# Adding x to the output rows: an accumulating transfer from DRAM in place of a load and GpSimd's additions

## Chip, cores and metric

The kernel runs on one core of one Trainium2 chip. The metric is the device time of one execution in microseconds (us). The engines are named as in the profile: PE is TensorE's matmul, PEld its weight load, DVE is VectorE, ACT is ScalarE, POOL is GpSimd, and SP is SyncE, which here only issues transfers. A "q" behind a name (SPq) stands for the engine's sequencer.

## What is computed

A cross attention over B = 64 independent items. Item b has text rows x[b] (256 x 512) and context rows c[b] (256 x 384). All is in float32.

```
text_p  = x @ W_text  + b_text           # 256 x 512
audio_p = ctx @ W_audio + b_audio        # 256 x 512
Q = layer_norm(text_p, g1, beta1);  K = layer_norm(audio_p, g2, beta2);  V = audio_p
alpha = softmax(Q K^T / sqrt(512))       # 256 x 256
H = (alpha V) @ W_out + b_out            # 256 x 512
out = layer_norm(H + x, g_out, beta_out)
```

The last line is the one that matters here: x itself is added to the projected rows, ahead of the last layer norm.

## The kernel before

Each item is 256 rows, so two blocks of 128 partitions (LT = ST = 2). The order of instructions on every engine is written out by hand; each engine works through its own queue in that order, and waits by semaphore where an operand isn't there yet. A loop over b = 0 to 61 runs three items at once in one iteration: the scores and softmax of item b, the projections q and k of item b + 2, and the context, output projection and last layer norm of the items before b. In an iteration `at` is the attention of item b, `last` that of b - 1 and `done` that of b - 2. The last two items run behind the loop in code of their own.

The projections q, k and the output projection y are objects of class `Blocks`: PE computes seven half-width products (`products`, line 472) into PSUM, and DVE brings them out one after the other (`leave`, line 483) in the order 1, 6, 2, 5, 3, 7, 4. After `leave(3)` row block 0 of the result is complete, after `leave(4)` row block 1.

q and k are turned by way of DRAM. SP stores the rows (`store`, line 418: tiles qr to qd, kr to kd), fetches them again in 32-row squares by four transfers each (`fetch`, by `squares` at line 88: qq, kq), and DVE transposes the squares (lines 91 and 439). The softmax weights e take the same way (ed, eq). x and c are read twice: in squares (xq, cq) for the projections, and in rows (`load_rows`, lines 113 and 114) for the addition of x and for the context product.

The rows of x, `x_sb`, are a 512 KB tile of pool `xin` (three buffers). Item 0 has its own loads at line 157. The output rows y, tile `yr` (two buffers), go through these steps for `done`, in three places of an iteration:

- DVE: `leave(3)`, `leave(7)`, `leave(4)`; then POOL: `add_x` (line 593), one addition for each of the two row blocks. Next in POOL's queue are `sum_x` and `sum_c` of item b + 3 (`turn_next`), whose results are used an iteration later, then the 1/std of y.
- ACT: `statistics` (lines 601 and 606), two passes over each row block, first the mean and then the centred square sum. They stand in ACT's queue behind the exponentials and the division of e, and ahead of the squares of q, the copies of the context zT and the affine steps of qT and kT.
- DVE: `shift` (line 694) and `settle` (line 703), which overwrite y in place; between them stands the transpose of k. Behind them on DVE come the seven `leave` steps of k, then those of the next y. SP: `store` (line 713) writes y to the output.

The four last items (60 to 63) are finished behind the loop. For items 62 and 63 the rows of x are used in other ways too: POOL adds the output bias into them (`add_bias`), and DVE adds them as it brings the product out of PSUM (`evict`).

Of the kernel before, what the change touches and what calls it, by code (L numbers as in the profile page):

```python
# [9 lines left out]
F32 = mybir.dt.float32  # L10
AF = mybir.ActivationFunctionType
ALU = mybir.AluOpType
# [3 lines left out]
P = 128  # L16
# [6 lines left out]
def kernel(  # L23
# [41 lines left out]
    nc = tc.nc  # L65
    ctx.enter_context(tc.manual_schedule())
    B, L, D = x.shape
    S, DA = c.shape[1:]
    H = w_text.shape[1]
    LT, ST = L // P, S // P  # L70
# [4 lines left out]
    xin = ctx.enter_context(tc.tile_pool(name="xin", bufs=3))  # L75
# [32 lines left out]
        load_x(b)  # L108

    def load_rows(b):  # L110
        x_sb = xin.tile([P, LT, D], F32, tag="x", name=f"x_{b}")
        c_sb = cin.tile([P, ST, DA], F32, tag="c", name=f"c_{b}")
        nc.sync.dma_start(x_sb, x[b].rearrange("(t p) d -> p t d", p=P))
        nc.sync.dma_start(c_sb, c[b].rearrange("(t p) d -> p t d", p=P))
        return x_sb, c_sb

# [382 lines left out]
    class Attention:  # L499
# [89 lines left out]
            self.y = self.o.rows  # L589

        def add_x(self):
            for t in range(LT):
                nc.gpsimd.tensor_tensor(self.y[:, t, :], self.y[:, t, :], self.xb[:, t, :], ALU.add)  # L593

# [261 lines left out]
    for b in range(B - 2):  # L856
# [23 lines left out]
        if b + 4 < B:  # L880
            load_squares(b + 4)
        at.fetch_e()
        rows[b + 1] = load_rows(b + 1)
        if done:
            done.statistics()
# [59 lines left out]
    q[B - 1].fetch()  # L945
    k[B - 1].fetch()
    rows[B - 1] = load_rows(B - 1)
    at.scores()
    done.o.leave(3)
# [107 lines left out]
```

## Time and profile before

| | |
|---|---|
| median of 3 runs | 1422.26 us (1420.84 to 1422.74) |
| the profiled execution | 1420.47 us, its span 1418.7 us, granted clock 0.998 |
| busy time: PE, DVE, ACT, POOL | 1405.0, 1273.3, 931.8, 875.2 us |
| DMA | 322.61 MB, mean 227 GB/s; SP's queue occupies 80.4% of the 16 DMA engines |
| x in rows (line 113) | 63 transfers of 512 KB, median 3.9 us from issue to landing |
| additions of x (line 593) | 124, mean 1274 ns, 157.0 us busy |
| POOL's idle time ahead of them | 58.0 us, ended by DVE's last writes of y |

The span is the time from the first to the last instruction in the profile; the execution's own time lies 1.8 us above it, and this execution lies 1.8 us below the median. Each row of the profile is of one execution. A row such as `L593 POOL TENSOR_TENSOR yr<-yr,x` gives the line of the kernel, the engine, the operation, and the tile written and those read. The mean granted clock is TensorE's, as a share of full speed. The time from issue to landing runs from the instruction that issues a transfer to its semaphore.

### The profile page before, as it was taken

How to read it: one execution, taken by the hardware profiler on the slowest of the kernel's cores; microseconds unless marked ns; L12 is line 12 of the kernel's file. 1: busy time of each engine (PE TensorE's matmuls, PEld its weight loads, DVE VectorE, ACT ScalarE, POOL GpSimd, SP SyncE). 2: the span in 40 equal slices, each digit the busy share in tenths (PEclk: the TensorE clock that was granted, in tenths of full speed). 3: DMA queues.
4: the chain of work that ended last, by engine and by line, in shares of the span. 5: the costliest groups of instructions: out<-in, count | busy, mean ns of one | idle time of the engine just before them, and what ended most of it. 6: DMA issues, size and time to landing. Idle time of an engine off the chain costs nothing.

```text
span 1418.7 us, 23330 instructions
## 1 busy us (share of the span) xinstructions
PE 1405.0 (99%) x6441; PEld 1220.9 (86%) x6441; DVE 1273.3 (90%) x2134; ACT 931.8 (66%) x2293; POOL 875.2 (62%) x1295
## 2 busy tenths in 40 slices
PE   9999999999999999999999999999999999999997
PEld 5788888888888888888888888888888888888885
DVE  5889999999999999999999999999999999999987
ACT  4666676676676676766766766766767667667662
POOL 5557556666666666566566665666665755666645
PEclk9999999999999999999999999999999999999999
DMA  8898887887888788788878887887887888788763
GB/s 207 228 246 229 242 244 209 242 240 216 237 233 234 228 230 238 233 226 236 244 217 236 239 224 228 238 229 229 229 238 232 225 239 242 216 238 241 205 200 109
DMA packets 450582, 322.61 MB, mean 227 GB/s; under 512 B 154900, under 2 KB 382996, under 8 KB 450452
## 3 DMA queue, kind: packets, MB, share of 16 engines
q1 hardware_dynamic: 450356, 320.98, 80.4%
q8 instruction: 53, 0.87, 0.3%
q14 instruction: 77, 0.63, 0.2%
q10 hardware_dynamic: 96, 0.13, 0.0%
HBM read 204.09 MB, written 116.92 MB: 226 GB/s over the span
## 4 chain that ended last, share of the span: by engine, by line
PE 94%; DMA 2%; DVE 1%; POOL 1%; SPq 1%; issue 1%; ACT 0%; POOLq 0%; DVEq 0%; ACTq 0%
PE ps_q L472 26%; PE ps_y L472 21%; PE ps_k L472 20%; PE ps_sc L511 15%; PE ps_z L577 11%; DMA qq<-qd 0%; DMA xq<-in_x_dram 0%; DMA qd<-qr 0%; DMA wt<-in_L_xattn_W_text_dram 0%; SPq L150 0%; DMA bt<-in_L_xattn_b_text_dram 0%; POOL rstd L343 0%; POOL ve L341 0%; DVE qr L483 0%; DVE st L267 0%
## 5 line engine op out<-in xcount | busy, mean ns | idle before, releaser
L341 POOL TENSOR_SCALAR ve<-var 128x2 f32<-128x2 f32 x126 | 43.6, 346 | 310.8 <-ACT junk L380 310.8
L511 PE MATMUL ps_sc<-kT,qT 128*128 128x256 f32 x1024 | 231.7, 379 | 1.9 <-ACT kT L446 1.9
L528 ACT ACTIVATE e<-ps_sc,nmx 128x256 f32<-128x256 f32 x128 | 59.5, 469 | 245.7 <-DVE nmx L521 245.7
L483 DVE TENSOR_TENSOR qr<-ps_q,qr 128x512 f32<-128x512 f32 x378 | 188.1, 511 | 35.8 <-PE ps_q L472 23.3
L511 PEld LDWEIGHTS ps_sc<-kT,qT 128*128 128x128 f32 x1024 | 194.2, 190 | 29.6 <-ACT kT L446 2.9
L483 DVE TENSOR_TENSOR kr<-ps_k,kr 128x512 f32<-128x512 f32 x378 | 188.2, 512 | 24.7 <-PE ps_y L472 0.5
L483 DVE TENSOR_TENSOR yr<-ps_y,yr 128x512 f32<-128x512 f32 x372 | 185.1, 511 | 24.1 <-DVE yr L483 0.9
L593 POOL TENSOR_TENSOR yr<-yr,x 128x512 f32<-128x512 f32 x124 | 157.0, 1274 | 58.0 <-DVE yr L483 58.0
L577 PE MATMUL ps_z<-eT,c 128*128 128x256 f32 x768 | 176.5, 379 | 0.1
L472 PE MATMUL ps_q<-wtsum,xsum 128*128 128x256 f32 x756 | 173.6, 379 | 0.0
L343 POOL TENSOR_TENSOR rstd<-ve,nhalf 128x2 f32<-128x2 f32 (+1 forms) x194 | 158.9, 819 | 16.1
L472 PE MATMUL ps_k<-wa,cT 128*128 128x256 f32 x630 | 166.8, 379 | 0.0
L472 PE MATMUL ps_y<-wao,zT 128*128 128x256 f32 x620 | 164.2, 379 | 0.0
L577 PEld LDWEIGHTS ps_z<-eT,c 128*128 128x128 f32 x768 | 145.8, 190 | 20.7 <-ACT e L528 0.5
L472 PEld LDWEIGHTS ps_q<-wtsum,xsum 128*128 128x128 f32 x756 | 143.6, 190 | 19.9 <-POOL xsum L305 0.5
L380 ACT ACTIVATE junk<-kr 128x512 f32<-128x512 f32 x126 | 79.3, 629 | 96.8 <-DVE kr L483 96.8
L446 ACT ACTIVATE qT<-qT,columns 128x256 f32<-128x256 f32 x256 | 132.8, 591 | 8.3 <-DVE qT L91 8.3
L472 PEld LDWEIGHTS ps_k<-wa,cT 128*128 128x128 f32 x630 | 119.6, 190 | 16.2
L446 ACT ACTIVATE kT<-kT,columns 128x256 f32<-128x256 f32 x256 | 132.2, 589 | 1.1 <-DVE kT L91 0.9
L472 PEld LDWEIGHTS ps_y<-wao,zT 128*128 128x128 f32 x620 | 117.7, 190 | 16.0
L408 ACT ACTIVATE kr<-kr,rstd 128x512 f32<-128x512 f32 x126 | 84.1, 714 | 69.9 <-POOL rstd L343 69.9
L703 DVE SCALAR_TENSOR_TENSOR yr<-yr,rstd,beo 128x512 f32<-128x512 f32 x124 | 127.4, 1065 | 0.6 <-POOL rstd L343 0.6
(150 smaller groups left out, 2946.4 us busy)
## 6 DMA issues: line engine op xcount, KB each, us to landing
kd<-kr SPq DMA_DIRECT2D x64, 512.0 KB, 3.1
kq<-kd SPq DMA_DIRECT2D x256, 128.0 KB, 3.4
qd<-qr SPq DMA_DIRECT2D x64, 512.0 KB, 5.1
qq<-qd SPq DMA_DIRECT2D x256, 128.0 KB, 3.3
xq<-in_x_dram SPq DMA_DIRECT2D x252, 128.0 KB, 2.9
x<-in_x_dram SPq DMA_DIRECT2D x63, 512.0 KB, 3.9
out_dram<-yr SPq DMA_DIRECT2D x62, 512.0 KB, 5.0
cq<-in_ctx_dram SPq DMA_DIRECT2D x252, 96.0 KB, 2.5
```

The source lines that it names most:

```text
L341: nc.gpsimd.tensor_scalar(ve, var, EPS, None, ALU.add)
L343: nc.gpsimd.tensor_tensor(r, ve, nhalf[:, :n], ALU.pow)
L380: nc.scalar.activation(junk, self.rows[:, t, :], AF.Square, scale=1.0 / math.sqrt(H), accum_out=self.var[:, t : t + 1],)
L408: nc.scalar.mul(row, row, self.r[t])
L446: nc.scalar.activation(self.T[:, k, :], self.T[:, k, :], AF.Identity, bias=bet[:, k : k + 1], scale=gam[:, k : k + 1],)
L472: nc.tensor.matmul(bank[:, j, :], lhsT=side, rhs=w, start=(i == 0), stop=(i == len(pairs) - 1))
L483: add = lambda o, i0, i1: nc.vector.tensor_tensor(o, i0, i1, ALU.add)
L511: nc.tensor.matmul(self.sc[:, t, :], lhsT=self.qT[:, k, bass.ts(t, P)], rhs=self.kT[:, k, :], start=(k == 0), stop=(k == HC - 1),)
L528: nc.scalar.activation(self.e[:, t, :], self.sc[:, t, :], AF.Exp, bias=self.nmx[:, t : t + 1], accum_out=self.den[:, t : t + 1],)
L577: nc.tensor.matmul(ps[:, j, :], lhsT=self.c_sb[:, s, bass.ts(lo + j, P)], rhs=self.eT[:, s, :], start=(s == 0), stop=(s == ST - 1),)
L593: nc.gpsimd.tensor_tensor(self.y[:, t, :], self.y[:, t, :], self.xb[:, t, :], ALU.add)
L703: nc.vector.scalar_tensor_tensor(self.y[:, t, :], self.y[:, t, :], self.r[t], beo_sb, ALU.mult, ALU.add)
```

## The change

For items 0 to 59 the tile of x in rows is no longer allocated and no longer loaded. Where POOL added it, POOL now issues one transfer that reads x[b] from DRAM and adds it to y in SBUF. It covers both row blocks, 512 KB. The items 60 to 63 keep the load and the additions, and item 0 keeps its own loads at line 157, since its projection needs them.

```diff
     def load_rows(b):
-        x_sb = xin.tile([P, LT, D], F32, tag="x", name=f"x_{b}")
         c_sb = cin.tile([P, ST, DA], F32, tag="c", name=f"c_{b}")
-        nc.sync.dma_start(x_sb, x[b].rearrange("(t p) d -> p t d", p=P))
+        x_sb = None
+        if b >= B - 4:
+            x_sb = xin.tile([P, LT, D], F32, tag="x", name=f"x_{b}")
+            nc.sync.dma_start(x_sb, x[b].rearrange("(t p) d -> p t d", p=P))
         nc.sync.dma_start(c_sb, c[b].rearrange("(t p) d -> p t d", p=P))
         return x_sb, c_sb
...
         def add_x(self):
+            if self.b < B - 4:
+                rows_of_x = x[self.b].rearrange("(t p) d -> p t d", p=P)
+                nc.gpsimd.dma_start(self.y, rows_of_x, accum_op=ALU.add)
+                return
             for t in range(LT):
                 nc.gpsimd.tensor_tensor(self.y[:, t, :], self.y[:, t, :], self.xb[:, t, :], ALU.add)
```

## The prediction

> **What bounds the kernel now.** I read the page first, then stretches, then one iteration in the timeline, then the DMA engines in half-microsecond steps.
>
> ```profile
> span 1418.7 us, 23330 instructions
> PE 1405.0 (99%) x6441; PEld 1220.9 (86%) x6441; DVE 1273.3 (90%) x2134; ACT 931.8 (66%) x2293; POOL 875.2 (62%) x1295
> ```
>
> PE is busy 99% of the span. The view of busy time in three stretches says where the missing 13.7 us lie (columns: stretch, its length, busy time of PE, PEld, DVE, ACT, POOL, granted clock, DMA share, GB/s).
>
> ```profile
> 0.00:61.47 61.47, 56.94 (x213) 38.89 (x213) 42.10 (x71) 30.45 (x71) 33.63 (x60) 1.00 0.87 212
> 61.47:1378.30 1316.83, 1316.83 (x6100) 1158.84 (x6101) 1199.14 (x2007) 889.88 (x2197) 819.33 (x1212) 1.00 0.82 232
> 1378.30:1418.70 40.40, 31.25 (x129) 23.18 (x128) 32.07 (x58) 11.47 (x26) 22.26 (x25) 0.93 0.37 115
> ```
>
> From 61.47 to 1378.30 PE is never idle, at full granted clock. All idle time lies in the start (4.5 us) and the end (9.2 us). The timeline shows the period of the loop, by the first of the score products:
>
> ```profile
> 83.34 3.62 PE L511 MATMUL ps_sc<-kT,qT 128*128 128x256 f32 x16
> 104.93 3.62 PE L511 MATMUL ps_sc<-kT,qT 128*128 128x256 f32 x16
> 126.51 3.62 PE L511 MATMUL ps_sc<-kT,qT 128*128 128x256 f32 x16
> ```
>
> One iteration is 21.58 us of matmuls without a gap. Other work costs time only when it comes too late for PE; then it costs its lateness every iteration. So the question is how late x may land in y. These are the timeline's rows around the addition (start, length, engine, line); all are of the iteration at 709 to 731, but the last two, which repeat the end of the DVE work one period later.
>
> ```profile
> 710.60 2.52 POOL L593 TENSOR_TENSOR yr<-yr,x 128x512 f32<-128x512 f32 x2 [0.94 <-DVE yr L483]
> 711.05 0.36 SPq L418 DMA_DIRECT2D kd<-kr  x1
> 711.50 2.40 SPq L88 DMA_DIRECT2D qq<-qd  x4
> 714.20 1.78 SPq L88 DMA_DIRECT2D kq<-kd  x4
> 717.05 0.61 ACT L601 ACTIVATE junk<-yr 128x512 f32<-128x512 f32 x1
> 718.27 0.71 ACT L606 ACTIVATE junk<-yr,nm 128x512 f32<-128x512 f32 x1
> 720.85 1.37 DVE L694 SCALAR_TENSOR_TENSOR yr<-yr,nm,go 128x512 f32<-128x512 f32 x2
> ...
> 732.93 0.42 DVE L483 TENSOR_TENSOR yr<-ps_y,yr 128x256 f32<-128x256 f32 x1
> 733.27 0.70 DVE L91 STREAM_TRANSPOSE eT<-eq 128x512 f32<-128x512 f32 x1
> ```
>
> Two additions run back to back, the first as soon as row block 0 is complete. ACT comes to its statistics of y (L601) only at 717.05, 3.9 us after the additions end (713.12), and has no idle time there. Last, the DMA engines where the transfer would flow:
>
> ```profile
> 711.50:712.00 0.50, 0.50 (x4) 0.45 (x3) 0.50 (x2) 0.00 (x0) 0.50 (x2) 1.00 0.11 41
> 712.00:712.50 0.50, 0.50 (x5) 0.42 (x4) 0.50 (x2) 0.00 (x0) 0.50 (x1) 1.00 1.02 389
> 713.00:713.50 0.50, 0.50 (x4) 0.45 (x3) 0.50 (x2) 0.00 (x0) 0.12 (x1) 1.00 1.00 213
> ```
>
> They wake at about 711.9 for kd and are then full.
>
> **What is removed.** 59 loads of x (63 less those of items 60 to 63; item 0 has its own), 120 of 124 additions. The additions are 120 x 1.274 = 153 us of POOL, which is 62% busy and waited for by nobody here: worth 0. The loads are 0.40 us of issue on SP, worth 0 as SP waits behind them for DVE and ACT rows anyway. On the DMA engines each is 512 KB at about 400 GB/s = 1.3 us, between 725 and 730.5. Behind it c, out and qd land up to 1.3 us sooner; qd lands at 727.11 + 5.1 = 732.2 as it is, before its readers issue at 733.09: worth 0.
>
> **What is added.** 60 accumulating transfers, at the same place in POOL's queue. Three things differ from the additions.
>
> First, release. One transfer covers both row blocks, so it waits for the last DVE write of y, which ends at 732.93 + 0.42 - 21.58 = 711.77, not 710.60. Behind it on POOL wait sum_x and sum_c of a later item (used an iteration later, so covered) and the 1/std of this y, before which POOL idles 1.24 us. Issuing may take 2.52 + 0.54 + 1.24 = 4.3 us before that is late: 0.
>
> Second, the landing becomes a wait of ACT at L601. Call the time from release to landing L. Up to 717.05 - 711.77 = 5.3 us it costs nothing. Then ACT is late, and queued behind L601 are the squares of q, the two copies of zT that feed POOL's sums and PE's y products, and the affine steps of qT and kT. The y products have slack: POOL's second sum ends at 723.75, and PE reads it at 705.81 + 21.58 = 727.39, so 3.6 us. DVE has less. Its shift (L694) overwrites y and must wait for L606 of row block 0, which ends 718.98, so landing to shift is 718.98 - 717.05 = 1.93 us (1.95 with block 1). From the shift at 720.85 DVE works without an idle gap through the k rows to the last write of y at 733.35, 12.50 us. That write releases the next transfer. So there is a loop: L + 1.95 + 12.50 = L + 14.45. While L is below 21.58 - 14.45 = 7.13 us, PE sets the period; above it the loop does, and each microsecond costs 60 us.
>
> Third, L itself. No accumulating transfer and no transfer issued by GpSimd is in this trace, so each part is bounded.
> - Release to first data: kd, issued by SP at 711.05, moves data at 711.9, so 0.85 at least. At most GpSimd needs as long to write its list of rows as it took to add them: 0.85 + 2.52 = 3.4. I take 2.1, since POOL's smaller instructions take 0.5 to 1.2 us.
> - Data: x must be read and y must be read and rewritten. One pass is 1.3 us, two are 2.6. The engines are full with kd, qq and kq (shares 1.00 to 1.02); taking equal turns doubles 2.6 to 5.2. I take 4.7, nearer to the full rows.
> - Last data to landing: kd's data ends about 713.2 and it lands at 711.05 + 3.1 = 714.15, so 0.9; for x, 0.6.
>
> L = 2.1 + 4.7 + 0.9 = 7.7, with ends 0.85 + 1.3 + 0.6 = 2.75 and 3.4 + 5.2 + 1.0 = 9.6. The lower end is as good as the plain load of x (3.9 from issue to landing). The period is 7.7 + 14.45 = 22.15, 0.57 more, times 60 is 34 us.
>
> By the Trainium skill (DMA: Bandwidth & Descriptors, section Latency and other measured facts) a GpSimd transfer's first byte comes about 1 us after issue against 0.6 for SP. Estimated from that page's difference, the first part would be 0.85 + 0.4 = 1.25, L 6.85, and nothing would be lost. The same page's fit (section Anatomy of one DMA — SWDGE (gpsimd) path: 2.0 us and the bytes by 436 GB/s) would give 3.2 us for 512 KB, which the plain load's 3.9 in this trace already exceeds. I keep the rows' sum.
>
> The new traffic also delays kd, qq and kq by up to its 2.6 us. The last qq is issued at 713.45 and lands 3.3 later at 716.75; DVE turns it at 719.69, so 2.9 us of cover. The last kq lands at 715.53 + 3.4 = 718.9 and is turned at 722.14: 3.2. So 0, with 0.3 us to spare; if ACT is late by over 1.6 us, kd starts late as well and this cover goes too, but then DVE is late by itself.
>
> **The sum.** 1420.47 (span 1418.7) + 34 = 1454.5; the median of the runs is 1.8 above the profiled execution: 1456.
>
> **Rivals.**
> - No change: L stays under 7.13. For it: the plain load's 3.9, and 5.3 us that cost nothing at all. Against it: two reads, a full DMA, a later release. Time 1422, its own range 1420 to 1424.
> - The DMA engines become the bound. They are busy 0.82 x 21.58 = 17.7 us an iteration, which leaves 3.9, and 1.3 comes free with x. An accumulation that occupies them over 5.2 us breaks the period. Two passes at the 213 GB/s row are 4.9, so it takes a slower one than any row of this size; at 7.2 us the time is 2.0 x 60 = 120 us more, 1542.
> - Faster: GpSimd has 153 us less to do. PE has no idle gap in the loop to give, and start and end keep their loads and additions. Some 2 us at the edges at most: 1420 or less.
>
> **Chances.** The landing loop 0.53; DMA-bound 0.12; no change 0.32; faster 0.03. About 0.2% (2.8 us) is what a measurement of this kernel can tell from no change. Faster 0.03, same 0.32, slower 0.65. The forecast's range by L from 7.2 to 9.3 is 1426 to 1552; with the no-change case, 1419.5 to 1550. It leaves out the upper part of the DMA-bound case (0.06), L over 9.3 (0.08) and most of faster (0.02).
>
> **What would show it.** In the changed profile: PE's score products 22.1 us apart instead of 21.58 and PE idle; ACT waiting at L601 for a DMA into yr, longest in the list of waits; landing 7 to 8 us after issue; POOL some 150 us less busy; x loaded 4 times in 512 KB pieces. An unchanged 21.58 with ACT waiting little at L601 makes the forecast wrong in L; a DMA share near 1 in all windows means the second rival; kq or qq as what DVE waits for means that I misjudged the cover of the other transfers.

## The result, and the profile after

The changed kernel takes 1462.55 us (median of 6 runs, 1456.86 to 1467.37) against 1421.81 us before: a ratio of 1.0286, 95% interval 1.0271 to 1.0300, 41 us more. The profiled execution took 1456.86 us with a span of 1455.1, so it is the fastest of the six; what the profile shows is 36.4 us of span.

First the page: span, busy time, the two DMA queues (packets, MB, share of 16 engines), and three groups of instructions.

```profile
span 1455.1 us, 23096 instructions
PE 1421.1 (98%) x6441; PEld 1214.4 (83%) x6441; DVE 1247.0 (86%) x2134; ACT 921.9 (63%) x2293; POOL 771.9 (53%) x1235
...
q1 hardware_dynamic: 434308, 290.04, 77.2%
q0 software_dynamic: 16320, 31.46, 14.5%
...
L607 ACT ACTIVATE junk<-yr 128x512 f32<-128x512 f32 x120 | 74.5, 621 | 157.6 <-DMA yr<-in_x_dram 157.6
...
L596 POOL DMA_DIRECT2D yr<-in_x_dram x60 | 76.0, 1266 | 132.4 <-DVE yr L485 127.3
L91 DVE STREAM_TRANSPOSE qT<-qq 128x1024 f32<-128x1024 f32 x64 | 79.6, 1244 | 68.8 <-DMA qq<-qd 68.8
```

GpSimd's transfers have a queue of their own, and it occupies the engines for 14.5% of the span: 0.145 x 1455.1 / 60 = 3.5 us of all 16 engines per transfer. Two waits are new: ACT for the landing in yr (157.6 us) and DVE for the fetch of q (68.8 us, against 2.4 before). The stretch of the loop shows PE no longer without gaps, and fuller DMA engines (columns as before the change):

```profile
61.47:1410.00 1348.53, 1330.53 (x6090) 1150.68 (x6090) 1168.77 (x1999) 877.19 (x2192) 715.39 (x1150) 1.00 0.94 225
```

The starts of the first score product of the items are no longer 21.58 us apart: of the 57 in the loop's middle the median is 22.09 and the mean 22.16, single ones lie between 21.58 and 23.21. 60 x (22.16 - 21.58) = 35 us is nearly the whole difference of the spans. One iteration in the timeline:

```profile
702.63 3.62 PE L513 MATMUL ps_sc<-kT,qT 128*128 128x256 f32 x16
...
702.83 3.26 DVE L485 TENSOR_TENSOR yr<-ps_y,yr 128x512 f32<-128x512 f32 x6
705.71 0.36 SPq L420 DMA_DIRECT2D kd<-kr  x1
706.16 2.37 SPq L88 DMA_DIRECT2D qq<-qd  x4
706.40 1.26 POOL L596 DMA_DIRECT2D yr<-in_x_dram  x1 [2.08 <-DVE yr L485]
708.86 2.62 SPq L88 DMA_DIRECT2D kq<-kd  x4
713.60 0.63 ACT L607 ACTIVATE junk<-yr 128x512 f32<-128x512 f32 x1 [2.13 <-DMA yr<-in_x_dram]
714.47 1.25 DVE L91 STREAM_TRANSPOSE qT<-qq 128x1024 f32<-128x1024 f32 x1 [0.76 <-DMA qq<-qd]
714.84 0.71 ACT L612 ACTIVATE junk<-yr,nm 128x512 f32<-128x512 f32 x1
715.67 1.46 DVE L700 SCALAR_TENSOR_TENSOR yr<-yr,nm,go 128x512 f32<-128x512 f32 x2
724.30 3.26 DVE L485 TENSOR_TENSOR yr<-ps_y,yr 128x512 f32<-128x512 f32 x6
```

The last write of y ends at 702.83 + 3.26 = 706.09, GpSimd issues at 706.40, and ACT starts its statistics at 713.60: 7.5 us after the write here, 7.9 in the median. The shift follows ACT's start by 2.07 us (2.08 in the median). But just ahead of the shift DVE stands for 0.76 us before the turn of q, for a fetch that was issued from 706.16 on, side by side with the new transfer.

Which of the two comes last can be read from the start times. ACT's first centred pass (L612) ends at 714.84 + 0.71 = 715.55, and the shift starts 0.12 us later; behind the start of the turn it starts 1.20 later. Over the 57 iterations the shortest delays are 0.13 us behind ACT's pass and 1.17 behind the start of the turn. In 44 iterations the shift starts at the first of these, so ACT, and with it the landing, is what it waited for last; in 13 it is the turn of q. The margin is small: 0.2 us in the median, 0.6 at most. In the kernel before, the shift follows the turn in all 57, and ACT's pass has been over for 1.86 us (median). So the landing does hold up DVE, and the fetch of q is close behind. Whether the loss needs both is a question for experiments.

### The profile page after: what moved, and what is told of

It is laid out like the page before. It is cut to its first block, busy times and chain, and to the rows that moved or that the text cites. A ratio compares the mean times of both kernels' runs of the same rounds, so it can differ in the third digit from the quotient of the medians.

```text
span 1455.1 us, 23096 instructions
## 1 busy us (share of the span) xinstructions
PE 1421.1 (98%) x6441; PEld 1214.4 (83%) x6441; DVE 1247.0 (86%) x2134; ACT 921.9 (63%) x2293; POOL 771.9 (53%) x1235
## 3 DMA queue, kind: packets, MB, share of 16 engines
q0 software_dynamic: 16320, 31.46, 14.5%
## 5 line engine op out<-in xcount | busy, mean ns | idle before, releaser
L607 ACT ACTIVATE junk<-yr 128x512 f32<-128x512 f32 x120 | 74.5, 621 | 157.6 <-DMA yr<-in_x_dram 157.6
L341 POOL TENSOR_SCALAR ve<-ssq 128x2 f32<-128x2 f32 x60 | 39.6, 660 | 242.6 <-ACT junk L612 242.6
L343 POOL TENSOR_SCALAR ve<-var 128x2 f32<-128x2 f32 x126 | 27.5, 218 | 224.8 <-ACT junk L382 219.7
L596 POOL DMA_DIRECT2D yr<-in_x_dram x60 | 76.0, 1266 | 132.4 <-DVE yr L485 127.3
L91 DVE STREAM_TRANSPOSE qT<-qq 128x1024 f32<-128x1024 f32 x64 | 79.6, 1244 | 68.8 <-DMA qq<-qd 68.8
```

The source lines that it names most:

```text
L91: nc.vector.transpose(dst.rearrange("p k (b j) -> p b k j", j=SQ), src.rearrange("p b (k i) -> p b k i", k=chunks),)
L341: nc.gpsimd.tensor_scalar(ve, var, 1.0 / D, EPS, ALU.mult, ALU.add)
L343: nc.gpsimd.tensor_scalar(ve, var, EPS, None, ALU.add)
L596: nc.gpsimd.dma_start(self.y, rows_of_x, accum_op=ALU.add)
L607: nc.scalar.activation(junk, self.y[:, t, :], AF.Identity, scale=-1.0 / D, accum_out=self.nm[:, t : t + 1])
```

## Two loops, and experiments that tell them apart

Each wait closes a loop over iterations. The *landing loop* is the one of the prediction: last write of y, landing, statistics, shift, DVE's work up to the next last write. The *fetch loop* runs by way of SP: kd is issued, qq behind it, DVE turns q when qq has landed, works through k, ACT normalises k, and the next kd is issued. A loop sets the period when none of its links has slack left. Adding up its stretches doesn't show that: from one event to the same event an iteration later they make the period in any kernel, slack included. In the kernel before, kd to the turn of q is 8.64 us in the median and the turn to the next kd 12.95, the 21.58 that PE sets; only the link from qq to the turn is loose, as DVE practically never waits there, while ACT waits for the k rows of DVE. In the changed kernel both waits have changed. The rows of the lists of waits, of the kernel before and then of the changed one (waiting line, releaser, total us, times, longest):

```profile
ACT junk L380 <- DVE kr L483: 96.8, 120, 1.5
...
DVE qT L91 <- DMA qq<-qd: 2.4, 2, 1.8
```

```profile
DVE qT L91 <- DMA qq<-qd: 68.8, 61, 2.3
...
ACT junk L382 <- DVE kr L485: 5.4, 15, 0.5
```

So in the changed kernel the fetch loop isn't closed by itself: ACT, late by the landing, mostly comes to the k rows after DVE is done with them, so that the landing makes kd late as well. A third explanation is that the 16 DMA engines simply have too much to do. Times below are medians with the ratio to the kernel before of the same chip; periods are means of the same 57 iterations.

**The landing alone, without the traffic.** The kernel before, with one tiny transfer added:

```diff
         xs[b] = sum_x(xT.pop(b))
+        if done:
+            nc.gpsimd.dma_start(
+                done.y[:, :, :16],
+                x[done.b].rearrange("(t p) d -> p t d", p=P)[:, :, :16],
+                accum_op=ALU.add,
+            )
```

> The kernel before (loads of x, POOL's additions) with one more, tiny accumulating transfer into y, 16 columns of each row block (16 KB), issued by GpSimd behind the four sums of x, so that its landing is the last thing ACT's statistics wait for; these 16 columns get x twice. Hardly any traffic, but a late landing. It is issued about 716.5 on the scale of the profile before and lands 2.5 to 4.5 us later, 7.2 to 9.2 us after DVE's last write of y. Landing-loop theory: period = that time + 2.0 + 12.5, so 21.7 to 23.7, a time of 1430 to 1545, 1480 for a landing of 3.5 us. Traffic theory: 1420 to 1426.

Measured: 1517.67 us, ratio 1.0671 (1.0655 to 1.0686). The list of waits of this kernel:

```profile
ACT junk L601 <- DMA yr<-in_x_dram: 210.5, 59, 4.3
DVE yr L694 <- ACT junk L606: 133.7, 58, 3.0
```

ACT waits for the landing in 59 iterations, and DVE at the shift for ACT in 58. In each of the 57 iterations in the middle the shift starts 0.18 us behind ACT's pass, where the kernel before leaves 1.86. So no slack is left between them: ACT's statistics start 8.86 us after the last write of y (median), the shift 2.13 later, DVE needs 12.12 from there to the next last write, and the median period is 23.13. The landing loop exists and sets the period when the landing is that late, with 16 KB moved.

**The traffic alone, without the landing.** In the changed kernel the transfer goes to a dead tile, between two additions of a constant row:

```diff
-                nc.gpsimd.dma_start(self.y, rows_of_x, accum_op=ALU.add)
+                nc.gpsimd.tensor_tensor(self.y[:, 0, :], self.y[:, 0, :], bo_sb, ALU.add)
+                nc.gpsimd.dma_start(wo_sb[:, :LT, :], rows_of_x, accum_op=ALU.add)
+                nc.gpsimd.tensor_tensor(self.y[:, 1, :], self.y[:, 1, :], bo_sb, ALU.add)
```

> The changed kernel with its accumulating transfer sent to a dead region of SBUF of the same size (the first half of the tile of W_out), issued at the same place, between two additions on POOL that give y a constant row (the output bias) in place of x; so x is left out of the result. Same bytes, same issue, but nobody waits for the landing. Landing-loop theory: ACT waits for nothing at its statistics, the period is 21.58, the time 1420 to 1426. Traffic theory: DVE still waits about 1 us an iteration for qq, the time is 1440 to 1465.

Measured: 1448.71 us, ratio 1.0187 (1.0172 to 1.0202), period 22.04. Nobody waits for the landing, and two thirds of the loss are still there. Three rows of its list of waits and two of its timeline:

```profile
ACT junk L382 <- DVE kr L485: 91.0, 120, 1.4
...
DVE qT L91 <- DMA qq<-qd: 50.2, 60, 2.3
...
PE ps_y L474 <- DVE kr L485: 14.4, 24, 2.0
```

```profile
704.33 0.36 SPq L420 DMA_DIRECT2D kd<-kr  x1
...
713.34 1.25 DVE L91 STREAM_TRANSPOSE qT<-qq 128x1024 f32<-128x1024 f32 x1 [0.68 <-DMA qq<-qd]
```

DVE waits for qq in 60 iterations, ACT for DVE's k rows in all, and SP issues kd 0.03 us behind ACT's last row of k: the fetch loop is closed. kd to the turn of q takes 9.16 us in the median, in place of 8.64. PE then waits for DVE to empty PSUM. The shift follows the turn in all 57 iterations, with ACT's pass long over. The fetch loop is enough by itself.

**All of the change, but the landing has an iteration of time.** Statistics, shift, settle and store of an item are done one iteration later (every second y lies in the dead tile of W_out):

```diff
-        if done:
-            done.statistics()
+        if old:
+            old.statistics()
...
-        done, last = last, at
+        old, done, last = done, last, at
```

> The changed kernel with statistics, shift, settle and store of an item's y done one iteration later at the same places of the queues (every second y lies in the dead tile of W_out, so that there are four buffers); the item that is over at the end is finished just behind the loop. Same transfers at the same moments, but their landing has 21 us more. Landing-loop theory: no wait of ACT for the landing, period 21.58, time 1422 to 1432, of which up to 8 us is the extra item at the end. Traffic theory: the period stays 22.1, the time 1455 to 1470.

Measured: 1465.18 us, ratio 1.0306 (1.0291 to 1.0322), period 22.13. ACT's wait is gone and the period is that of the changed kernel. My theory of the landing loop fails here as the whole account of the loss: without that loop the loss is the same, but for 0.03 us an iteration, which is 2 us in all. DVE's wait for qq remained, nearly as large as in the changed kernel:

```profile
DVE qT L91 <- DMA qq<-qd: 64.6, 59, 2.0
```

And ACT waits for DVE's k rows again (83.9 us, 118 times), so without the landing the fetch loop closes and takes its place.

The time is above the changed kernel's although the period isn't, since the extra item at the end costs some 8 us: PE waits 8.0 us once for the transposed e there.

**Two transfers by row block.**

```diff
-                nc.gpsimd.dma_start(self.y, rows_of_x, accum_op=ALU.add)
+                for t in range(LT):
+                    nc.gpsimd.dma_start(self.y[:, t, :], rows_of_x[:, t, :], accum_op=ALU.add)
```

> The accumulation of each item as two transfers of 256 KB, one for each row block. Landing-loop theory (the time from DVE's last write of y to the landing, plus 2.08 us to the shift, plus 11.9 to 12.5 us of DVE work to the next last write of y, sets the period): block 0 is released 1.2 us earlier and has half the data, block 1 has half the data behind it. ACT's first pass starts 1 to 2 us sooner after the last write of y, 6 to 7 us in place of 7.9. The period falls to 21.6 to 21.7, the time to 1422 to 1430. Traffic theory (the added DMA work makes kd, qq and kq late, and DVE waits for them): the bytes are the same, so 1455 to 1465; and POOL issues twice, 2.5 us in place of 1.26, which could make it a little worse.

Measured: 1443.38 us, ratio 1.0154 (1.0138 to 1.0171), period 21.93. Neither number that was expected: ACT starts 5.28 us after the last write in the median, as in the kernel before, and still half of the loss remains, with DVE waiting 42.0 us for qq. The shift follows the turn of q in 56 of the 57 iterations, so what is left is the fetch's. How much of the gain comes from the earlier landing and how much from the earlier traffic isn't shown.

**A plain transfer in its place.**

```diff
-                nc.gpsimd.dma_start(self.y, rows_of_x, accum_op=ALU.add)
+                nc.gpsimd.dma_start(self.y, rows_of_x)
```

> The changed kernel with a plain transfer in place of the accumulating one, same place and size: x overwrites y, so the projection is left out of the result. Theory of two loops (landing: last write of y to ACT's statistics, plus 2.1, plus 11.9 to 12.2; fetch: kd's issue to the turn of q, which waits for qq behind it in the queue, plus 12.7): a plain transfer reads 512 KB less, so it lands 5.5 to 6.5 us after its start in place of 7.6, which takes the landing loop under 21.58, and qq comes back by 1.3 us or more, under 8.8 after kd: 1421 to 1430. If it is GpSimd's way of issuing (1.26 us of POOL and its own queue) and not the adding, the time stays 1450 to 1465.

Measured: 1423.24 us, ratio 1.0016 (1.0007 to 1.0025). Same queue, same bytes from DRAM, same wait, and the loss is all but gone: each of the 57 periods is 21.58. The rows of its page for GpSimd's queue and for the issue:

```profile
q0 software_dynamic: 8640, 31.46, 8.1%
...
L596 POOL DMA_DIRECT2D yr<-in_x_dram x60 | 47.9, 798 | 144.7 <-DVE yr L485 144.7
```

The engines are occupied 0.081 x 1422.8 / 60 = 1.9 us per transfer, against 3.5 for the accumulation; it lands 6.1 us after its start, against 7.6. The price of the change is thus the adding, not GpSimd's queue. The Trainium skill (Collectives: The Full Stack, section The bandwidth ceiling: the fold count and why AG ≠ RS ≠ AR) explains a reducing collective's lower rate by its two source reads and shows a ratio of 1.93 between a copying and an adding collective. Here the occupation by accumulating and plain transfers has a ratio of 3.5 / 1.9 = 1.8, which is near it; that the second read is the reason here too, no run shows.

**Three kernels with the fetch of q moved ahead of kd**, to break the fetch loop. The edit is the same in all; the kernels are the traffic-only one, the late one and the split one.

```diff
-            q[b + 1].fetch()
             k[b + 1].fetch()
...
         k2.normalise()
+        q2.fetch()
         k2.store()
```

> The traffic-only kernel (transfer into the dead tile, POOL adds the output bias in place of x) with the fetch of q moved ahead of the store of kd in SP's queue, so that qq no longer starts behind kd and beside the whole accumulation. Two-loops theory: the fetch loop is broken, the landing loop does not exist here, so the period is 21.58 and the time 1420 to 1428. Theory that the 16 DMA engines have too much to do (share 0.94): the order changes nothing, 1440 to 1450.

> The changed kernel with the statistics one iteration later and the fetch of q ahead of the store of kd: both loops broken, all the traffic and the accumulation into y kept. Two-loops theory: period 21.58 in the loop, time 1426 to 1434 (the extra item at the end costs about 8). Full DMA engines: 1455 to 1465.

> The accumulation in two transfers by row block (which brought ACT's statistics back to 5.3 us after the last write of y in its median) and the fetch of q ahead of the store of kd. Two-loops theory: both loops are at or under 21.58, time 1421 to 1432, the rest from iterations where block 1 lands late. Full DMA engines: 1440 to 1446 as without the move.

Measured: 1569.82 (ratio 1.1040, 1.1011 to 1.1068), 1579.05 (1.1122, 1.1089 to 1.1154) and 1551.32 us (1.0912, 1.0896 to 1.0928). All much slower, and neither theory had that. The list of waits of the traffic-only kernel, then of its SP queue:

```profile
DVE kT L441 <- DMA kq<-kd: 160.6, 60, 4.0
```

```profile
SPq L88 <- DMA kd<-kr: 377.8, 64, 7.9
SPq L88 <- DMA qd<-qr: 320.4, 64, 6.7
```

SP now stands before the fetch of q for qd's landing, with the store of kd queued behind it, and kd then shares the engines with qq and the accumulation (it lands after 6.8 us in place of 3.1), so kq, which must wait for kd, is what comes late. The move made a third loop in place of the second; it decides nothing about the second.

**The traffic moved in time.** The traffic-only kernel with its transfer issued behind the sums on POOL, some 7 us later, where the squares for a later item are being fetched:

```diff
             turn_next(b + 3)
+        if done and done.b < B - 4:
+            rows_of_x = x[done.b].rearrange("(t p) d -> p t d", p=P)
+            nc.gpsimd.dma_start(wo_sb[:, :LT, :], rows_of_x, accum_op=ALU.add)
```

> The traffic-only kernel (accumulation into the dead tile, POOL adds the output bias in place of x) with the transfer issued behind the sums of x and c on POOL, about 7 us later in the iteration, when qq and kq have been fetched and the squares of x and c for a later item are under way. The move of the fetch ahead of kd had failed as a test, since it put a wait for qd in front of kd and so made kq late; this one leaves SP's order alone. Fetch-loop theory: qq and kq are back at the turn in time, DVE waits for neither, period 21.58, time 1420 to 1428. Full DMA engines (0.94 to 0.96 busy whatever the order): 1440 to 1450.

Measured: 1422.22 us, ratio 1.0002 (0.9994 to 1.0011), each of the 57 periods 21.58. Its stretch of the loop and its rows for the two fetches (count, size, median from issue to landing):

```profile
61.47:1378.30 1316.83, 1315.46 (x6086) 1157.38 (x6087) 1197.76 (x2004) 890.28 (x2196) 890.78 (x1273) 1.00 0.95 231
```

```profile
kq<-kd SPq DMA_DIRECT2D x256, 128.0 KB, 3.4
...
qq<-qd SPq DMA_DIRECT2D x256, 128.0 KB, 3.2
xq<-in_x_dram SPq DMA_DIRECT2D x252, 128.0 KB, 6.2
```

The engines are 0.95 busy, as in the slow kernels, and nothing is lost: the explanation by full DMA engines falls. Now the fetches of x land late (6.2 in place of 2.9) and have an iteration to spare, and those of q and k are back at 3.2 and 3.4.

**Both at once, nothing left out.** The late kernel with its accumulation moved in the same way:

```diff
             done.o.leave(4)
-            done.add_x()
...
             turn_next(b + 3)
+        if done:
+            done.add_x()
```

> The kernel with the statistics one iteration later, the accumulation into y now issued behind the sums on POOL as in the traffic-only kernel of this set, and the steps of the extra item at the end put behind those of the next one. Nothing is left out: all accumulations, no wait for the landing, no collision with qq. Two-loops theory: 21.58 in the loop, time 1422 to 1430. Full DMA engines: 1450 to 1465.

Measured: 1427.78 us, ratio 1.0035 (1.0021 to 1.0049). Its loop is at 21.58 in each of the 57 periods; what is over comes from the extra item behind the loop, where the stretch from 1378.3 on is 47.7 us long instead of 40.4. With the late landing harmless and the traffic elsewhere, the accumulation costs nothing per iteration.

**Half of it.** SP loads the rows of block 1 alone, and block 0 gets x by the transfer:

```diff
+            nc.sync.dma_start(x_sb[:, 1, :], x[b, P:])
...
+                nc.gpsimd.dma_start(self.y[:, 0, :], rows_of_x[:, 0, :], accum_op=ALU.add)
+                nc.gpsimd.tensor_tensor(self.y[:, 1, :], self.y[:, 1, :], self.xb[:, 1, :], ALU.add)
```

> Half of the change: row block 0 gets x by an accumulating transfer of 256 KB, row block 1 by POOL's addition from a loaded half tile. Two-loops theory: the transfer is released 1.2 us earlier and occupies the engines about 1.8 us in place of 3.5, so it lands before ACT comes to its statistics, and qq is late by less than its cover: 1420 to 1426. If any accumulation costs in proportion to its bytes: half of the loss, 1440.

Measured: 1423.12 us, ratio 1.0013 (1.0004 to 1.0021). Half the bytes cost not half the loss but hardly anything: the price has a threshold, as both loops say. ACT waits 3.5 us in all for this transfer. No version beat the kernel before; its loop has no gap in PE to give back.

## Why the prediction was right, and where it was not

Forecast 1456, measured 1462.55; the loss was put at 34 us and is 41 in the median and 36 in the profiled execution. The reading of the profile held in most of its steps:

- PE sets the period of 21.58 and the 153 us of POOL are worth nothing: POOL is 103 us less busy (issuing takes 76) and no version is faster.
- The release waits for DVE's last write: POOL stands 127.3 us for it, in place of 58.0.
- The landing loop is at work in the changed kernel: ACT waits for the landing in all 57 iterations, the shift for ACT in 44, and the period is 22.16, as forecast (22.15).
- Its terms are off both ways, so that the sum fits this well is in part luck. L was put at 7.7 and is 7.9 in the median (7.97 in the mean). By the packets of GpSimd's queue, its parts are 2.9 us from release to first data, 4.5 of data and 0.5 to the landing, against 2.1, 4.7 and 0.9: the first was put 0.8 too short, the others together 0.6 too long. The other estimate of the first part, 1.25, by which nothing would have been lost, was further off. Landing to shift was 1.95 and is 2.08 (mean 2.11). The DVE stretch was 12.50 and is 11.9 (mean 12.10), mostly since the settle takes 1.37 where the row of before had 2.06.
- The rival of full DMA engines is refuted by the moved transfer, which keeps them 0.95 busy at no loss.

The step that failed is the cover of the other transfers: "So 0, with 0.3 us to spare". The accumulation was taken to occupy the engines 2.6 us, two passes of a plain one. It occupies them 3.5, more than the 2.9 us of cover that the turn of q had, and DVE now waits for qq 61 times. The prediction had named this sign of a misjudged cover itself. Priced at nothing, this step alone costs 27 us (the traffic-only kernel), and with the landing dependency taken away but the transfer at its real place, behind the last write of y, nearly the whole of the loss in the loop (the late kernel).

So the landing loop, which carried the forecast, is a real mechanism, but the loss doesn't need it. It is mostly last at the shift, by 0.2 us, and the fetch loop, which was left out of the sum, gives 22.13 in its place (the late kernel); lifting the landing alone therefore gained nothing. The prediction's remark that kd starts late as well when ACT is over 1.6 us late, "but then DVE is late by itself", fits what is seen: ACT waits 2.5 us for the landing in the median, and at the shift the fetch adds only 0.04 us to the mean iteration on top of it. What it missed is that the fetch comes late without the landing too. The number came out right without the fetch loop because the two happen to be nearly equally long; that wasn't foreseen, so this too is luck. What a kernel would take that had only the landing loop at this L was not tried. An estimate from its stretches in the changed kernel, L at its mean and the others at their shortest, is 7.97 + 2.07 + 11.89 = 21.93, or 21 us in 60 iterations.

## What to carry to other kernels

Where one engine sets the period without a gap, look for every loop that the change touches, not for the one that it lengthens: a new transfer has a landing that someone waits for, and a place in time at which it delays the transfers beside it. Write each loop as a sum of its links without their slack, each the shortest time from one release to the next, and compare it with the period (with the slack in them the stretches add up to the period in any kernel). In a profile, look at each place where two of them meet for the one that came last. A change is free as long as every loop stays below the period, and costs the excess in every iteration above it. Before giving up such a transfer, move it to where its neighbours have slack: the same bytes cost 27 us at one moment and nothing 7 us later.

## What the runs showed of the hardware

- An accumulating transfer of 512 KB from DRAM into SBUF occupies the 16 DMA engines 3.5 us and lands 7.6 us after GpSimd starts on it; a plain one from the same queue 1.9 and 6.1. GpSimd is occupied 1.27 and 0.80 us by the issue.
- Of the accumulating transfers the profile counts 16320 / 60 = 272 packets each, of the plain ones 8640 / 60 = 144, for the same 31.46 MB in all.
- The first packet of the accumulating transfer in the changed kernel moves 2.6 us after GpSimd starts the issue, and the last one ends 0.5 us before the landing (medians).
- An accumulating transfer of 16 KB, in 256 runs of 64 bytes, still takes 1.25 us to issue and lands 4.0 us after its start (median): 32 times fewer bytes, but over half of the time.
